# How two attentions of a four-layer graph kernel begin: tile 0's logits and search in a new order, and the second attention's first logits made at the end of the stage ahead

## The chip, the cores and the metric

The kernel runs on one core of a Trainium2 chip. The metric is the time on the device in microseconds (us). The profile is one execution, taken by the hardware profiler; its engines are TensorE (PE, with PEld for its weight loads), VectorE (DVE), ScalarE (ACT), GpSimd (POOL) and SyncE (SP), which issues most of the DMAs.

## The reference

3327 nodes have 256 features each. Four graph layers follow each other, each as `x = layernorm(x + layer(x, adj))`. The change lies in the fourth, which takes two steps of diffusion and of top-p attention:

```python
def top_p_attention(X):                      # W1, W2, W3: 64-wide projections
    q, k = X @ W1.T @ W2.T, X @ W3.T
    probs = softmax(q @ k.T)                 # 3327 x 3327
    sorted by size, row by row: keep an entry while the sum of the larger ones < 0.9
    A = probs * keep
    return A / max(A.sum(-1), 1e-12)
R = (S + I) / rowsum
Xf = Xa = X
for n in range(2):
    A = top_p_attention(Xa)
    Xf, Xa = R @ Xf, A @ Xa
    Z += Xf @ U1[n].T + Xa @ U2[n].T
return layernorm(X + Z)
```

## The kernel before, in words

The nodes are padded to 3328 and lie in `nt` = 26 tiles of 128 rows, with `half` = 1664 columns on either side and `nh` = 13 pairs of tiles. One tile of attention goes through these steps:

- *logits*: `scores` (L1141) makes a row of 3328 logits in four groups. A group is two matmuls (two of 416 columns, from either half of the row) into a PSUM buffer named `sc`, of which there is one, and a copy by ScalarE into the tile `e`. Before that GpSimd sets the one column of padding in `e` (L1146). In the second attention (`p` is 1) matmul and copy are kept in the order in which the program lists them, and each is a step of its own.
- *search*: which entries of `e` are kept. `search_short` (L1390), for the first attention, takes the top 8 of each of 26 segments of 128 (VectorE's MAX8 into `cand`), then six rounds of top 8 and match-replace on these, one exponential over the row by ScalarE after the first round, and the crossing of 0.9, found with a scan. Two maskings of 1664 columns follow. `search_long` (L1424), for the second, finds a cut by sums and counts: two exponentials, then `Relu` and `Sign` passes of ScalarE with an accumulated sum at a first cut c1, again at c2, and scalar steps between them on GpSimd; at c3 VectorE masks into `z`, takes segment maxima, six ranking rounds, the crossing, a match-replace and a masking.
- *products*: the finished `e` is transposed by TensorE, copied by ScalarE into `wt`, and multiplied into an accumulator `acc`. In the first attention two tiles go together with seven products in place of eight (`attended_pair`, with sums of blocks `b` of `X`, for which VectorE makes four of 128 x 1664 into `G`, used there as scratch); in the second one by one (`attended`, L1321).
- *ends*: `first` (L1553) multiplies a tile's result by the U and key matrices: it makes `Y`, the sum `s` (stored to DRAM as `sd`), the tile of `G` for the second attention, and the second attention's keys `kT` and queries `q` (stored as `qd`). `G`'s tile is stored to DRAM (`gd`) too, and read back as a whole into `G` after the first attention, in two loads on SyncE's queue.

Between these lie the products of the diffusion, from blocks of the transposed adjacency (`at`) that SyncE loads: one tile (`diffused_first`, for tile 1, called the x products below), then pairs (`diffused_pair`, with VectorE's subtraction `cb` for each load, and with `own_part`, GpSimd's scaling of a tile of X into `F`), in the second attention tile by tile (`diffused`, L1305, whose `t` and `s` GpSimd adds).

The order on each engine is written out by hand with generators: each of the parts yields after a step, and the main program draws on them in turn. `look` is one step of the oldest search in the queue. At the beginning of the first attention the program draws x products and groups of tile 0's logits by turns; then tile 0's search joins the queue, pair 1's diffusion is begun and its first `at` parts are asked for, and the rest of the x products go with tile 1's logits and two looks each. The loop over pairs follows. The second attention is a loop over `i` from -2 to 26: in round `i` tile `i + 2` has its logits made, tiles `i + 1` and `i` are searched and tile `i - 1` is multiplied. In rounds -2 and -1 there is little or nothing to multiply. Two aids fix an order: `here` and `keep_in_program_order` tie an instruction to its place on its engine; elsewhere a scheduler may move it.

Of the kernel before, what the change touches and what calls it, by code (L numbers as in the profile page):

```python
# [18 lines left out]
P = 128  # L19
# [31 lines left out]
def gnn_kernel(ctx: ExitStack, tc: tile.TileContext, n: int, a: dict, out: bass.AP):  # L51
# [816 lines left out]
    with tc.tile_pool(name="l3", bufs=1) as pool, tc.tile_pool(name="l3d", bufs=1, space=DRAM) as dram:  # L868
# [269 lines left out]
        def in_order(op):  # L1138
            return lambda *x, **k: tc.keep_in_program_order(op(*x, **k))  # L1139

        def scores(work, psum, p, q, e):  # L1141


            copy = in_order(nc.scalar.copy) if p else nc.scalar.copy
            if npad > n:
                nc.gpsimd.memset(e[:, n:], NEG)  # L1146
            halves = e.rearrange("p (h c) -> p h c", h=2)
            for c0 in range(0, half, KC):
                pl = psum.tile([P, 2, 512], F32, name="sc", bufs=1)
                ws = [min(KC, n - c0 - h * half) for h in range(2)]  # L1150

                for h, w in enumerate(ws):
                    k = slice(h * DA, (h + 1) * DA)
                    mm = tensor.matmul(pl[:, h, :w], q[k, :], kT[p][k, c0:c0 + w], start=True, stop=True)  # L1154
# [150 lines left out]
        def diffused(work, atp, psum, p, it, out, each=J3):  # L1305

            rd = rdeg[:, it:it + 1]
            t = work.tile([P, D], F32, name="t")
            nc.gpsimd.tensor_scalar(t, (Y if p else X)[:, it, :], rd, None, op0=ALU.mult)
            if p:  # L1310
                s = work.tile([P, D], F32, name="s")
                nc.sync.dma_start(s, sd[it])
                nc.gpsimd.tensor_tensor(t, t, s, op=ALU.add)
            for acc in aggregated(atp, psum, it, Y if p else X, each):
                if acc is None:
                    yield
            d = work.tile([P, D], F32, name="xf", bufs=DL + 3)
            nc.vector.scalar_tensor_tensor(d, acc, rd, t, op0=ALU.mult, op1=ALU.add)
            out.append(d)

# [61 lines left out]
        def t1(sm, name, w=1):  # L1382
            return sm.tile([P, w], F32, name=name)
# [37 lines left out]
        junks = [None]  # L1421
        edge = [None]

        def search_long(work, sm, e, total, v, kept, halves=False):  # L1424

# [1 line left out]

            def t(name):  # L1430
                return t1(sm, name)

            m8, neg, root = t1(sm, "m8", 8), t1(sm, "neg", 2), t("root")
            nc.vector.max(m8, e[:, :KC])
# [22 lines left out]
            f1, sg, k1, m1 = t("fs1"), t("sg"), t("k1"), t("m1")  # L1457
# [3 lines left out]
            here(nc.scalar.activation(junk, e, AF.Sign, bias=c1, scale=-1.0, accum_out=sg))  # L1461
# [19 lines left out]
            with tc.issue_after(second_cut.ins):  # L1481
# [8 lines left out]
            here(nc.scalar.activation(junk, e, AF.Sign, bias=c2, scale=-1.0, accum_out=sg))  # L1490
            yield
            x, c3 = t("x"), t("c3")
            nc.vector.reciprocal(s, s)
# [59 lines left out]
        def first(work, psum, it, acc, f, xf, tag="pj", xa=None):  # L1553
# [22 lines left out]
            for k in range(2):  # L1576
                tensor.matmul(pg[:, 0, :], xt[:, 2 + k, :], u2[:, 1, k, :], start=(k == 0), stop=(k == 1))
            project_keys(pg[:, 1, :P], it, xt[:, 2:, :])
            g = G[:, it, :] if tag == "pj" else work.tile([P, D], F32, name="s")
            nc.scalar.copy(g, pg[:, 0, :])  # L1580
            if tag != "pj":
                nc.sync.dma_start(gd[it], g)
            store_keys(work, pg[:, 1, :P], 1, it)
            yield
# [70 lines left out]
        with tc.tile_pool(name="l3w", bufs=2) as work, tc.tile_pool(name="l3s", bufs=4) as sm:  # L1655


            def start(p, t, es, searches, search):
                if p or t:
                    q = work.tile([2 * DA, P], F32, name="q")  # L1660
                    nc.sync.dma_start(q, qd[p][t])
                else:
                    q = q0
                es[t] = work.tile([P, npad], F32, name="e", bufs=4)
                searches[t] = search(work, sm, es[t], *(x[p][:, t:t + 1] for x in (tots, vs, kepts)),
                                     **({"halves": True} if p and t == nt - 1 else {}))
                return scores(work, psum, p, q, es[t])

            with tc.tile_pool(name="l3p", bufs=2, space=PSUM) as psum, tc.tile_pool(name="l3a", bufs=1) as quads:
                fixed = True  # L1670
# [56 lines left out]
                        next(todo[r][0])  # L1727
                    ends[0] = todo[0][0]

                groups = logits(0)  # L1730
                x = diffused_first(quads, psum, 1, xfs)
                for _ in groups:
                    next(x)
                queue.append(searches[0])
                spread = spreading(1)
                groups = logits(1)
                for _ in x:
                    next(groups, None)
                    looks(2)
                for _ in groups:  # L1740
                    pass
                queue.append(searches[1])
# [2 lines left out]
                for i in range(nh - 1):  # L1745
                    stage(spread, 7, logits(2 * i + 2), ends, counts,
                          {0: lambda: end_pair(i - 1) if i else None, 5: lambda: attend_to(i), 6: go_on})
                    go_on()
                    counts = [1, 2, 2, 2, 2, 0, 0]
                    queue.append(searches[2 * i + 2])  # L1750
                    values = turned[0]
                    for k in range(7):
                        next(values)
                        looks(k in (1, 2, 4, 5, 6))
                    stage(spread, 6, logits(2 * i + 3), todo[1], [2, 1, 2, 1, 2, 1], {})
                    finish()
# [14 lines left out]
                for it in (nt - 2, nt - 1):  # L1771
# [14 lines left out]
                        pass  # L1786
                    ends = first(quads, psum, it, acc, f, xfs[it], "tp", c)
                    next(ends)
                both(ends)
                fl0 = unresolved(sm, psum, 0)  # L1790
                fixed = False
            for x in (slice(0, JH), slice(JH, nt)):
                nc.sync.dma_start(G[:, x, :], gd[x].rearrange("t p d -> p t d"))

            with tc.tile_pool(name="l3q", bufs=3, space=PSUM) as psum, tc.tile_pool(name="l3at", bufs=3) as atp, \
                    tc.tile_pool(name="l3b", bufs=2) as lone:
                es, searches, xfs = {}, {}, []  # L1800
# [210 lines left out]
```

## Time and profile before

| | |
|---|---|
| median of 3 runs | 3396.89 us (3396.72 to 3399.24) |
| the profiled execution's own time | 3392.58 us |
| its span | 3390.8 us |
| mean granted TensorE clock | 0.967 of full speed |
| instructions | 50286 |

The page's rows are read like this: in the list of engines, the busy time, its share of the span and the number of instructions; in the rows of digits, 40 equal slices of the span, each digit the busy share in tenths (PEclk is the granted clock). The chain of work that ended last has these lines at its head:

```
PE 16%; DVE 4%; ACT 3%; POOL 2%; issue 1%; DMA 0%; SPq 0%; DVEq 0%; POOLq 0%
PE acc L1344 6%; PE acc L1299 6%; PE sc L1154 2%; PE tp L1330 2%; ACT junk L1477 1%; DVE cand L1356 1%; ACT junk L1490 1%; DVE z L1506 1%; DVE e L1535 1%; DVE top L1367 0%; DVE rest L1369 0%; ACT junk L1461 0%; ACT e L1139 0%; DVE e L1543 0
```

It is followed back only to 2557 us. Line 891 is that of a helper which issues the instructions of the first attention; there the tile's name and not the line tells which step it is. In the table of busy time by stretch the columns are the stretch, its length, the busy time of PE, PEld, DVE, ACT and POOL (with the number of instructions in brackets), the granted clock, the DMA engines' busy share and GB/s.

### The profile page before, as it was taken

What the parts mean: (1) busy time and instruction counts of PE and PEld (TensorE: products, weight loads), DVE (VectorE), ACT (ScalarE), POOL (GpSimd) and SP (SyncE); (2) the same over time, 40 slices, a digit from 0 to 9 for tenths busy, and PEclk for the clock granted to TensorE, in tenths of its full rate; (3) what the DMA queues carried; (4) which work ended last, traced back from release to release, by engine and by line L of the source; (5) the groups of instructions that cost most, each with busy time, mean ns of one, the idle gap of its engine ahead of it and who ended that gap; (6) DMA issues with size and microseconds to landing.
All of it is one profiled execution on the core that took longest, in us unless ns stands there. A gap on an engine that the chain in (4) does not pass through costs nothing. (4 is left out here: it accounts for less than half of the span.)

```text
span 3390.8 us, 50286 instructions
## 1 busy us (share of the span) xinstructions
PE 3121.1 (92%) x18301; PEld 2560.0 (75%) x18301; DVE 2692.5 (79%) x5899; ACT 1730.8 (51%) x2763; POOL 1133.6 (33%) x1328
## 2 busy tenths in 40 slices
PE   8999888988888766999979999999997899999997
PEld 5999656666676555888858898898885677777776
DVE  4665268999999998777578878878854899999996
ACT  1000556767667676111133433433436888888883
POOL 0000245656666655111220000000003566666663
PEclk9999999998999888999989999999998999999999
DMA  6775334333343221444322322322313122222221
GB/s 200 250 257 191 112 98 121 114 108 110 103 118 98 63 61 46 167 143 151 118 79 85 89 73 81 89 73 81 89 41 108 42 68 69 66 59 73 72 63 35
DMA packets 206264, 344.31 MB, mean 102 GB/s; under 512 B 22222, under 2 KB 129166, under 8 KB 205870
## 3 DMA queue, kind: packets, MB, share of 16 engines
q1 hardware_dynamic: 205998, 340.92, 33.1%
q8 instruction: 148, 2.42, 0.3%
q14 instruction: 118, 0.97, 0.1%
HBM read 304.65 MB, written 36.21 MB: 101 GB/s over the span
## 5 line engine op out<-in xcount | busy, mean ns | idle before, releaser
L330 POOL TENSOR_TENSOR h<-du,row 128x2048 f32<-128x2048 f32 (+1 forms) x110 | 465.9, 4235 | 344.7 <-DVE hc L330 243.0
L330 DVE TENSOR_TENSOR_SCAN h<-dA,carry,h 128x512 f32<-128x512 f32 (+1 forms) x384 | 448.8, 1221 | 21.7 <-ACT dA L337 21.5
L337 ACT ACTIVATE dA<-t,A_log 128x512 f32<-128x512 f32 (+1 forms) x448 | 292.6, 658 | 147.7 <-DVE h L330 146.0
L1299 PE MATMUL acc<-F,at 128*128 128x256 f32 x1352 | 345.4, 384 | 3.0 <-DMA at<-in_adjT 2.1
L1344 PE MATMUL acc<-G,wt 128*128 128x256 f32 x1352 | 332.6, 388 | 8.6 <-ACT wt L1139 8.3
L1079 PE MATMUL acc<-F,at 128*128 128x257 f32 x1352 | 302.1, 380 | 0.8 <-ACT r L1023 0.8
L389 PE MATMUL cb<-F,at 128*128 128x256 f32 x1196 | 293.0, 393 | 7.6 <-ACT hn L409 3.4
L1344 PEld LDWEIGHTS acc<-G,wt 128*128 128x128 f32 x1352 | 248.9, 191 | 65.3 <-ACT wt L1139 35.5
L1299 PEld LDWEIGHTS acc<-F,at 128*128 128x128 f32 x1352 | 241.8, 191 | 53.6 <-issue 21.5
L1079 PEld LDWEIGHTS acc<-F,at 128*128 128x128 f32 x1352 | 252.4, 190 | 36.1 <-issue 1.1
L680 PE MATMUL y<-ident,hc 128*128 128x128 f32 x1664 | 235.9, 296 | 45.7 <-DVE hc L330 45.5
L1146 POOL MEMSET e<- 128x1 f32 x52 | 4.9, 99 | 816.2 <-PE tp L891 752.5
L680 PEld LDWEIGHTS y<-ident,hc 128*128 128x128 f32 x1664 | 209.4, 153 | 86.6 <-DVE hc L330 62.1
L389 PEld LDWEIGHTS cb<-F,at 128*128 128x128 f32 x1196 | 228.7, 197 | 58.8 <-issue 20.4
L330 DVE TENSOR_TENSOR hc<-h,row 128x2048 f32<-128x2048 f32 (+2 forms) x114 | 243.0, 2133 | 9.7 <-PE y L680 2.6
L891 PE MATMUL acc<-X,at 128*128 128x128 f32 (+1 forms) x988 | 173.7, 287 | 6.1 <-issue 6.1
L1263 ACT COPY wt<-tp 128x512 f32<-128x512 f32 x156 | 90.7, 591 | 167.1 <-PE tp L891 151.7
L138 PE MATMUL acc<-t,cb 128*128 128x128 f32 (+1 forms) x1014 | 168.4, 275 | 0.0
L891 PEld LDWEIGHTS acc<-X,at 128*128 128x128 f32 x988 | 142.3, 194 | 30.1 <-issue 25.3
L891 PE MATMUL acc<-G,sw 128*128 128x128 f32 x936 | 155.5, 275 | 0.0
L1160 ACT COPY e<-sc 128x832 f32<-128x832 f32 x78 | 65.9, 845 | 174.8 <-PE sc L891 174.7
L891 DVE MAX8 cand<-e 128x8 f32<-128x128 f32 x676 | 139.8, 278 | 5.5 <-ACT e L1160 3.7
(417 smaller groups left out, 7273.0 us busy)
## 6 DMA issues: line engine op xcount, KB each, us to landing
at<-in_adjT SPq DMA_DIRECT2D x54, 832.0 KB, 4.4
at<-in_adjT SPq DMA_DIRECT2D x130, 320.0 KB, 3.0
row<-bc SPq DMA_DIRECT2D x80, 512.0 KB, 4.9
at<-in_adjT SPq DMA_DIRECT2D x52, 640.0 KB, 5.3
at<-in_adjT SPq DMA_DIRECT2D x52, 576.0 KB, 4.3
at<-in_adjT SPq DMA_DIRECT2D x72, 256.0 KB, 3.1
at<-mixed SPq DMA_DIRECT2D x72, 256.0 KB, 3.6
mixed<-cb SPq DMA_DIRECT2D x26, 640.0 KB, 3.9
```

The costliest lines, as they stand in the source:

```text
L138: mm = nc.tensor.matmul(acc, w[:, j, :], x, start=(y == 0 and k % 3 == 0 and k < 6), stop=(y == nh - 1 and k in (2, 6)))
L330: return lambda *x, **k: tc.keep_in_program_order(op(*x, **k))
L337: decays.append(op(*x, **k))
L389: ten.matmul(acc, at[:, j % JC, :], X0[:, j, :], start=(j == 0), stop=(j == nt - 1))
L680: x = ten.matmul(y[:, g * P:(g + 1) * P], h[:, g, i * P:(i + 1) * P], ident, is_transpose=True, start=(first and g == 0), stop=(last and g ...
L891: return lambda *x, **k: tc.keep_in_program_order(op(*x, **k))
L1079: nc.tensor.matmul(acc, at[:, j, :], F[:, j0 + j, :], start=(j0 + j == 0), stop=(j0 + j == nt - 1))
L1146: nc.gpsimd.memset(e[:, n:], NEG)
L1160: copy(halves[:, :, c0:c0 + ws[0]], pl[:, :, :ws[0]])
L1263: nc.scalar.copy(wts[-1], pt)
L1299: nc.tensor.matmul(acc, at[:, j, :], rhs[:, j0 + j, :], start=(j0 + j == 0), stop=(j0 + j == nt - 1))
L1344: tensor.matmul(acc, wt[:, j, :], rhs[:, j0 + j, :], start=(j0 + j == 0), stop=(j0 + j == nt - 1))
```

## The change

In the first attention:

- `scores` takes a list of PSUM names; tile 0's groups use `sc` and `acc` by turns. All of its groups are made before the x products; then tile 0's search joins the queue.
- One group of tile 1's logits goes with every second part of the x products, and three looks with every part. Pair 1's diffusion is begun after the x products. So the seven parts hold 21 looks, tile 0's whole search.
- A copy by ScalarE into a small tile `ex` is written ahead of it all.

In the second attention:

- Tile 0's logits are made in the end of the first attention: two steps of them with each step of the last tile's `first`.
- The last four tiles' part of `G` is written by ScalarE straight to its place, without the store to DRAM; the loads of the other 22 are moved ahead of the last pair's ends.
- Rounds -2 and -1 of the loop are replaced by a written list: who takes a step (tile 0's search, tile 1's search, or None for tile 1's logits) and how many diffusion products follow. Products in the list count 26.
- In tile 0's search the two `Sign` passes of ScalarE become counts on VectorE, each in two half passes with an accumulated sum and two small steps.
- The tile `xf` of the diffusion has one more buffer.

```diff
+        def scores(work, psum, p, q, e, banks=("sc",)):
...
+            for k, c0 in enumerate(range(0, half, KC)):
+                bank = banks[k % len(banks)]
+                pl = psum.tile([P, 2, 512], F32, name=bank, bufs=1 if bank == "sc" else 2)
...
+            def signs(c):
+                ks, sg = t1(sm, "ks", 2), t("sg")
+                if counted:
+                    for h in range(2):
+                        z = lone.tile([P, half], F32, name="z", bufs=1)
+                        nc.vector.tensor_scalar(z, e[:, h * half:(h + 1) * half], c, 0.0, op0=ALU.is_gt, op1=ALU.add,
+                                                accum_out=ks[:, h:h + 1])
+                    nc.vector.tensor_add(sg, ks[:, :1], ks[:, 1:])
+                    nc.vector.tensor_scalar(sg, sg, -2.0, float(npad), op0=ALU.mult, op1=ALU.add)
+                else:
+                    here(nc.scalar.activation(junk, e, AF.Sign, bias=c, scale=-1.0, accum_out=sg))
+                return sg
...
-            g = G[:, it, :] if tag == "pj" else work.tile([P, D], F32, name="s")
+            direct = tag == "pj" or it >= nt - 4
+            g = G[:, it, :] if direct else work.tile([P, D], F32, name="s")
             nc.scalar.copy(g, pg[:, 0, :])
-            if tag != "pj":
+            if not direct:
                 nc.sync.dma_start(gd[it], g)
...
-                groups = logits(0)
+                nc.scalar.copy(small.tile([P, 1], F32, name="ex"), eps_t)
                 x = diffused_first(quads, psum, 1, xfs)
-                for _ in groups:
-                    next(x)
+                for _ in logits(0):
+                    pass
                 queue.append(searches[0])
+                groups = logits(1)
+                for k, _ in enumerate(x):
+                    if k % 2 == 0:
+                        next(groups, None)
+                    looks(3)
                 spread = spreading(1)
-                groups = logits(1)
-                for _ in x:
-                    next(groups, None)
-                    looks(2)
...
+                for x in (slice(0, JH), slice(JH, nt - 4)):
+                    nc.sync.dma_start(G[:, x, :], gd[x].rearrange("t p d -> p t d"))
                 end_pair(nh - 2)
...
-                both(ends)
+                es, searches = {}, {}
+                groups = start(1, 0, es, searches, search_long)
+                for _ in ends:
+                    next(groups)
+                    next(groups)
+                both(groups)
...
-            for x in (slice(0, JH), slice(JH, nt)):
-                nc.sync.dma_start(G[:, x, :], gd[x].rearrange("t p d -> p t d"))
...
+                groups = start(1, 1, es, searches, search_long)
+                for t, products in ((0, 0), (0, 0), (None, 0), (None, 4), (0, 0), (None, 0), (None, 4),
+                                    (0, 0), (0, 0), (None, 0), (None, 4), (0, 0), (None, 0), (None, 4),
+                                    (0, 0), (1, 0), (1, 4), (0, 0), (0, 6)):
+                    next(groups if t is None else searches[t], None)
+                    for _ in range(products):
+                        next(spread)
-                for i in range(-2, nt + 1):
+                for i in range(nt + 1):
...
-                    share = iter(range(shares[i - 1] if 0 < i < nt else nt if -2 < i < 1 else 0))
+                    share = iter(range(shares[i - 1] if 0 < i < nt else nt if i < 1 else 0))
```

The instructions on each engine stand in the new order in the two beginnings alone; TensorE has three more of 6381 in the fourth layer. From the first attention's loop over pairs to the last pair's ends, and from the second attention's round 1 on, the order is the same in both.

More of the change, by code (lines that the diff above doesn't have):

```diff
@@ L1139, in in_order @@
             return lambda *x, **k: tc.keep_in_program_order(op(*x, **k))
-        def scores(work, psum, p, q, e):
+        def scores(work, psum, p, q, e, banks=("sc",)):
             copy = in_order(nc.scalar.copy) if p else nc.scalar.copy
@@ L1147, in scores @@
             halves = e.rearrange("p (h c) -> p h c", h=2)
-            for c0 in range(0, half, KC):
-                pl = psum.tile([P, 2, 512], F32, name="sc", bufs=1)
+            for k, c0 in enumerate(range(0, half, KC)):
+                bank = banks[k % len(banks)]
+                pl = psum.tile([P, 2, 512], F32, name=bank, bufs=1 if bank == "sc" else 2)
                 ws = [min(KC, n - c0 - h * half) for h in range(2)]
@@ L1316, in diffused @@
                     yield
-            d = work.tile([P, D], F32, name="xf", bufs=DL + 3)
+            d = work.tile([P, D], F32, name="xf", bufs=DL + 4)
             nc.vector.scalar_tensor_tensor(d, acc, rd, t, op0=ALU.mult, op1=ALU.add)
@@ L1422, in gnn_kernel, with search_long @@
         edge = [None]
-        def search_long(work, sm, e, total, v, kept, halves=False):
+        def search_long(work, sm, e, total, v, kept, halves=False, counted=False):
             def t(name):
                 return t1(sm, name)
+            def signs(c):
[10 more added lines that the diff above has]
+                return sg
             m8, neg, root = t1(sm, "m8", 8), t1(sm, "neg", 2), t("root")
@@ L1456, in search_long @@
             inverse(rc, c1)
-            f1, sg, k1, m1 = t("fs1"), t("sg"), t("k1"), t("m1")
+            f1, k1, m1 = t("fs1"), t("k1"), t("m1")
             yield
@@ L1460, in search_long @@
             yield
-            here(nc.scalar.activation(junk, e, AF.Sign, bias=c1, scale=-1.0, accum_out=sg))
+            sg = signs(c1)
             yield
@@ L1489, in search_long @@
                 scaled(level, c2, float(npad), level, ALU.mult, ALU.add)
-            here(nc.scalar.activation(junk, e, AF.Sign, bias=c2, scale=-1.0, accum_out=sg))
+            sg = signs(c2)
             yield
@@ L1665, in start @@
                 searches[t] = search(work, sm, es[t], *(x[p][:, t:t + 1] for x in (tots, vs, kepts)),
-                                     **({"halves": True} if p and t == nt - 1 else {}))
-                return scores(work, psum, p, q, es[t])
+                                     **({"halves": t == nt - 1, "counted": t == 0} if p else {}))
+                return scores(work, psum, p, q, es[t], ("sc", "acc") if not p and t == 0 else ("sc",))
             with tc.tile_pool(name="l3p", bufs=2, space=PSUM) as psum, tc.tile_pool(name="l3a", bufs=1) as quads:
@@ L1788, in gnn_kernel @@
                     next(ends)
[L1789 removed]
+                es, searches = {}, {}
[4 more added lines that the diff above has]
+                both(groups)
                 fl0 = unresolved(sm, psum, 0)
                 fixed = False
[L1792 to L1793 removed]
             with tc.tile_pool(name="l3q", bufs=3, space=PSUM) as psum, tc.tile_pool(name="l3at", bufs=3) as atp, \
                     tc.tile_pool(name="l3b", bufs=2) as lone:
[L1800 removed]
+                xfs = []
                 result = iter(())
```

## The prediction

> **What bounds the kernel now.** I read the page first, then busy time by stretch, then TensorE's waits at each attention's beginning, then the time lines of the engines that it waits for.
>
> ```profile
> PE 3121.1 (92%) x18301; PEld 2560.0 (75%) x18301; DVE 2692.5 (79%) x5899; ACT 1730.8 (51%) x2763; POOL 1133.6 (33%) x1328
> PE   8999888988888766999979999999997899999997
> PEclk9999999998999888999989999999998999999999
> ```
>
> The first attention runs from 1698 to 2547 us, the second from there to the end. A slice is 84.8 us: in PE's row the two beginnings are slices 21 (7) and 32 to 33 (7, 8), all others of the attentions are 9. Busy time by stretch says it sharper:
>
> ```profile
> 1690.00:1753.00 63.00, 42.74 (x218) 29.79 (x216) 39.72 (x113) 18.44 (x23) 27.25 (x29) 0.88 0.33 100
> 1753.00:2500.00 747.00, 746.62 (x5823) 669.39 (x5823) 615.48 (x2077) 283.22 (x456) 3.31 (x25) 1.00 0.26 77
> 2535.00:2680.00 145.00, 115.95 (x502) 81.70 (x500) 81.81 (x242) 103.29 (x97) 58.39 (x124) 0.91 0.25 78
> 2680.00:3360.00 680.00, 671.66 (x3264) 511.56 (x3263) 622.54 (x1855) 559.76 (x551) 421.69 (x818) 1.00 0.22 65
> ```
>
> The second number is the stretch, the third PE's busy time. After each beginning PE is full, and from there on both kernels issue the same instructions in the same order. So what a beginning gains goes through to the end; it holds 20 us of idle PE in the first, 29 in the second. PE's waits name them:
>
> ```profile
> PE tp L891 <- DVE e L891: 10.1, 2, 8.7
> PE tp L1330 <- DVE e L1543: 12.5, 3, 9.2
> PE sc L1154 <- ACT q L907: 2.3, 1, 2.3
> ```
>
> Columns: total, times, longest. The long waits are those for the first finished weights: tile 0's and 1's e in the first attention (PE idle from 1742.6), tile 0's e in the second (idle from 2607.9).
>
> **First attention, part by part.** The logits of tile 0 take a second PSUM name by turns, and all four groups stand ahead of the x products (tile 1's diffusion), which before waited for the same stream: x's first load lands at 1705. ScalarE's copies (0.85 us each, first at 1700.34) so end at 1703.7 instead of 1717.0. VectorE is in its four products for G until 1708.03; its first 25 segment maxima (0.20 each) end at 1713.1. The 26th needs the padding column, and that is a new gate:
>
> ```profile
> 1690.01 26.22 POOL L1203 TENSOR_SCALAR F<-X,rdeg 128x256 f32<-128x256 f32 x23
> 1716.18 0.18 POOL L1146 MEMSET e<- 128x1 f32 x4
> 1742.64 0.38 DVE L891 MAX8 top<-cand 128x8 f32<-128x208 f32 x1
> 1749.21 1.95 DVE L891 SCALAR_TENSOR_TENSOR e<-e,v 128x1664 f32<-128x1664 f32 x1
> ```
>
> Start, duration, engine. The memset queues behind 23 scalings and ends at 1716.3, hidden before. Tile 0's top then starts at 1716.6, where it was 1720.0. Tile 1's rows give the rest of a search: top 1742.64 to first masking 1749.21 is 6.57 us with one cb subtraction in it, 5.97 without; two maskings (1.87 pitch) follow. Tile 0's search is now whole, ahead of F and cb: 1716.6 + 5.97 + 3.75 and small steps = 1726.6. Then F (0.49) and two cb (0.69 each): 1728.4. Tile 1's maxima take 5.2: 1733.6; 6.57 more: masking from 1740.2, ended at 1742.1 and 1744.0, against 1751.3 and 1753.1. **9.1 us.** ScalarE's copies of tile 1 are done by then, and PE's own work from 1697.9 (11 logits groups at 0.9, 52 products at 0.206, 6 pair products at 1.56: 30 us) would end at 1728 if never kept waiting, so VectorE's chain decides. It keeps PE waiting in new places: pair 1's first product needs cb, now at 1727.7, some 2 us after tile 1's logits, and the fifth needs the third cb at 1736.9, behind two rounds of tile 1's search. PE then ends its queue at 1740.8 and idles 3 us, not 8.7.
>
> Here a clock loss goes too: after the idle from 1742.6 the granted clock was 0.5 from 1747.8 to 1757.5, about 1.9 us of slower matmuls behind 1753. The clock fell 5.2 us after the stop here, 3.7 us after it at 2607.9; a stop of 3 us should not reach it. **11.0 us** in all; bounds 9 (clock lost as before) and 13 (memset no gate).
>
> The copy to "ex", which uses ScalarE before the logits, is placed by the scheduler far ahead, in layer 1; the activation table load stays in front of the first e copy (1699.05 to 1700.33). I cost it at nothing (0.2 us of ScalarE at 51% busy), and it gains nothing.
>
> **Second attention.** Before, after the last tile's U matmuls (2541.12), PE stood 2.28 us for that tile's q (ScalarE first waited 2.33 us at 2546.71 for buffer s, whose reader is a store) and began tile 0's logits at 2547.71, four groups at 2.7 us each through one PSUM buffer; copies ended at 2557.70. Now two groups are issued while PE waits for xt and for F, one each after; the last four tiles' G goes straight to its place, so neither store nor wait is left. With matmul groups of 0.9 and copies of 0.85: groups at 2540.3, 2543.8, 2546.1, 2548.05, e at 2550.0, **7.7 us earlier**. The four stores and their wait are gone; G's load moves ahead on SP's queue, behind the store of tile 21 and nothing later, so nothing behind it stalls. Before, it occupied the DMA engines when the first at block was asked for at 2550.66 (0.94 and 0.92 busy in 2550 to 2560), and that landed at 2559.4; with the queues clear, 3.0 us is the median of such a load: 2553.5.
>
> The search: exponentials (3.07 + 0.19 each) 2550.1, 2554.1 to 2557.3, c1 at 2557.8. Before, Relu waited in ScalarE's order for tile 1's copies until 2569.66, and Sign followed it. Now Relu (2558.05 to 2561.3) runs beside the count on VectorE in two half passes. No row shows this form at that width: the near row is the masking of 128x1664, 1.95 us, the other end the same operation at 128x104, 0.32 us, scaled by width less a fixed 0.16: 2.6. I take 1.95, as it reads one stream to the row's two. Count ends at 2562.3. POOL's steps to c2 took 3.5 us undisturbed (2601.75 to 2605.2): 2565.9. On ScalarE tile 1's exponential now lies ahead of Relu(c2): 2567.2 to 2570.4, and the second count ends with it. Then c3, 2.0 as before, and z at 2573.1 (before 2590.4). z and the maxima took 9.1 us before (2590.38 to 2599.92, less a diffusion row of 0.47): the six ranking rounds start at 2582.3 and five of them are over at 2586.3.
>
> Here comes the wait that takes the place of the removed ones:
>
> ```profile
> 2606.33 0.16 DVE L1493 RECIPROCAL s<-s 128x1 f32<-128x1 f32 x1 [2.03 <-POOL s L1447]
> ```
>
> That reciprocal is tile 1's, stands in VectorE's queue ahead of tile 0's last steps in both kernels, and waits for POOL's s, so for tile 1's exponentials, Relu and Sign on ScalarE. Queued behind it: the crossing, match-replace and masking of tile 0, and PE's transposes behind them. From tile 1's earlier start I work out Sign at 2584.3, c2 at 2588, s behind POOL's t (0.94) at 2590.2; then 10.5 us as before (2606.33 to 2617.05, less a diffusion row): e at 2600.7, **16.3 us earlier**.
>
> That holds with a warm PE. The trace speaks against it:
>
> ```profile
> 2545.00:2550.00 5.00, 1.72 (x11) 0.81 (x11) 0.78 (x4) 1.74 (x4) 0.00 (x0) 0.98 0.21 66
> 2550.00:2555.00 5.00, 3.10 (x10) 0.59 (x8) 0.25 (x1) 1.70 (x2) 2.12 (x3) 0.50 0.94 308
> ```
>
> PE busy 1.72 of 5.00, then clock 0.50, until 2563.8. [...] By the row a thinly used stretch is enough. After the change PE has only two groups and a few projections in 2546 to 2551 and stays as thin. I go by the row: half clock from 2551 to 2563 costs the 16 products among tile 1's logits their 0.206 once more (3.3 us) and the logits some 0.4, so 3.7 us, on tile 1's s, and e is at 2604.4: **12.7 us**. Bounds: 7.7 (only the logits' head start survives) and 19 (no wait at the reciprocal).
>
> Behind tile 0's e the order is the old one. The next waits (59.65 us from there to tile 2's e, through ScalarE's queue) start earlier by the same amount.
>
> **Sum** against the profiled execution, 3392.58 (span 3390.8 and 1.8 around it): 11.0 + 12.7 = 23.7, so 3368.9. It lies 4.3 below the median, 3396.89; the predicted median is 3373.2. The measurement tells 0.2% apart, 6.8 us.
>
> **Rivals.**
> - *Warm* (0.15). PE keeps its full clock in both: 11 + 16.3 to 19, so 27 to 30: 3367 to 3370. [...] Against: the row.
> - *One beginning only* (0.22). The cb held back behind tile 0's search starves the pair products, or PE falls cold and only 9 us or less is left of the first; or in the second tile 1's s stays near 2606.3. Gain 9 to 14: 3383 to 3388. For: each beginning already ends in a wait that the change moves by order alone. Against: the 30 us of PE work leave 12 us of room.
> - *Nothing* (0.06). The shift is absorbed behind: some later chain (the 59.65 us with ScalarE's queue) is bound to what did not move. 3390 to 3397. Against: 746.62 of 747 and 671.66 of 680 busy.
> - *Slower* (0.04): VectorE's reciprocal for tile 1. Tile 1's logits, products and loads start inside cold PE and share ScalarE with tile 0's passes; each us that tile 1's s is late is a us of e. The gain is gone at 2606.3; with the first's 11, the kernel is slower from 2617, and measurably from 2624, 20 us later than worked out at half clock. At 2630 it would be 3410. Against: in the kernel before, with tile 1's loads landing later, it was ready at 2606.3.
>
> **Numbers.** My case has 0.53. Range 3363 to 3387: the low end is both upper bounds (13 + 19 = 32, with 2 for a shared error), the high end a gain of 10. Faster 0.90, same 0.06, slower 0.04.
>
> **What would show it.** Right: tile 0's top in the first attention within 1 us of 1716.6, set by the memset; PE's wait for tile 0's and 1's e 3 us; clock 1.0 in 1740 to 1755; in the second, e's copies done 7 to 8 us earlier, PE at half clock shortly after, VectorE's longest wait at tile 1's reciprocal, tile 0's e at 2604 less the first's 11; PE full behind both. Wrong: a second PSUM buffer that makes PE wait elsewhere, a count pass of over 3 us, or a wait for tile 2's e that grows by what tile 0's lost.

## The result, and the profile after

The changed kernel took 3375.79 us, median of 4 runs (3371.59 to 3379.24); the kernel before, on the same chip, 3396.8 us, median of 4 (3391.59 to 3399.24). The ratio is 0.9943, with a 95% interval of 0.9929 to 0.9956: 15 to 24 us faster, 19.4 in the middle. The forecast was 23.7 us, the time 3373.2 us.

The profiled execution took 3376.88 us with a span of 3375.1, only 15.7 us less than that of before. The reason for the small difference is in front of the change: VectorE's last F row, with which the layers ahead end, starts at 1699.66 us here and at 1697.01 before. Over all traces below it lies between 1692.4 and 1701.6, with nearly the same code ahead of it. So I compare stages, from marks that lie inside the fourth layer.

The page of the changed kernel, the same rows as before:

```profile
PE 3123.7 (93%) x18301; PEld 2564.2 (76%) x18301; DVE 2700.0 (80%) x5911; ACT 1723.8 (51%) x2760; POOL 1127.4 (33%) x1328
PE   8999888988888767899989999999998899999997
PEclk9999998999999888999999999999999999999999
```

PE's busy time is the same to 2.6 us, as nothing was taken from it; what fell is its idle time. The longest waits of PE in the first beginning (1690 to 1900 us), then those in the second (2510 to 2680), with two lines of the kernel before under the first:

```profile
PE sc L891 <- ACT e L1161: 6.4, 2, 4.7
PE acc L891 <- DVE cb L891: 3.9, 1, 3.9
PE acc L891 <- issue: 2.2, 1, 2.2
PE sc L891 <- DVE F L931: 1.2, 1, 1.2
PE tp L891 <- DVE e L891: 0.5, 1, 0.5
...
PE acc L891 <- issue: 6.1, 1, 6.1
PE sc L891 <- ACT e L1160: 3.1, 2, 2.2
```
```profile
PE tp L1331 <- DVE e L1557: 9.3, 3, 4.3
PE acc L1345 <- ACT wt L1139: 4.1, 3, 1.7
PE acc L1300 <- DMA at<-in_adjT: 3.1, 1, 3.1
PE acc L1300 <- issue: 2.8, 1, 2.8
```

The 10.1 us for the first weights are 0.5, and the 6.1 us for the first load of x are 2.2. In their place the wait for ScalarE grew from 3.1 to 6.4, and the 3.9 for cb is new. In the second, the 12.5 us for finished weights became 9.3: tile 0's part fell from 9.2 to 2.2, but tile 1's rose from 0.6 to 2.8 and tile 2's from 2.7 to 4.3. The 2.3 for q are gone.

The stages, each mark taken as a start: F (that last row), sw (the first product with sw), tp (the last tile's transposes from sw), e0 (the first transposes of the second attention's tile 0).

| us | F to sw | sw to tp | tp to e0 | e0 to end |
|---|---|---|---|---|
| before | 62.88 | 780.0 | 77.20 | 773.7 |
| changed | 55.94 | 780.0 | 63.35 | 776.15 |

The middle is equal to 0.1 us, in every trace: what the first beginning gains goes through. In this pair of traces the gain is 6.9 us in the first and 11.4 from tp on: 13.85 at e0, of which 2.45 are lost again behind it.

### The profile page after: what moved, and what is told of

It reads as the page before. It is cut to its first block, busy times and chain, and to the rows that moved or that the text cites. A ratio compares the mean times of both kernels' runs of the same rounds, so it can differ in the third digit from the quotient of the medians.

```text
span 3375.1 us, 50279 instructions
## 1 busy us (share of the span) xinstructions
PE 3123.7 (93%) x18301; PEld 2564.2 (76%) x18301; DVE 2700.0 (80%) x5911; ACT 1723.8 (51%) x2760; POOL 1127.4 (33%) x1328
## 5 line engine op out<-in xcount | busy, mean ns | idle before, releaser
L389 PEld LDWEIGHTS cb<-F,at 128*128 128x128 f32 x1196 | 231.0, 199 | 60.1 <-issue 20.4
L1444 ACT ACTIVATE junk<-e,c 128x3328 bf16<-128x3328 f32 x50 | 154.1, 3083 | 0.0
```

What stands on the lines that cost most here:

```text
L389: ten.matmul(acc, at[:, j % JC, :], X0[:, j, :], start=(j == 0), stop=(j == nt - 1))
L1444: here(nc.scalar.activation(junk, e, AF.Sign, bias=c, scale=-1.0, accum_out=sg))
```

## The experiments

The table gives each kernel's time, and its stages from one trace; e1 to e4, e5 to e8 and e9 to e12 shared a chip each. The scatter of times is such that ratios tell about 4 us apart; the stages of the first attention repeat within 1.4 us with equal code there (54.8 to 56.1).

| | median us | ratio to before, 95% | F to sw | tp to e0 | tp to end |
|---|---|---|---|---|---|
| e1 first part only | 3384.54 | 0.9976 (0.9969 to 0.9983) | 55.16 | 78.11 | 852.9 |
| e2 second part only | 3378.61 | 0.9968 (0.9958 to 0.9978) | 62.04 | 62.49 | 836.4 |
| e3 padding on VectorE | 3369.90 | 0.9937 (0.9924 to 0.9949) | 50.05 | 65.34 | 840.5 |
| e4 x products ahead | 3371.30 | 0.9946 (0.9930 to 0.9961) | 53.15 | 62.85 | 838.0 |
| e5 Sign on ScalarE | 3378.54 | 0.9954 (0.9941 to 0.9967) | 54.81 | 65.44 | 837.0 |
| e6 G by DRAM | 3371.87 | 0.9935 (0.9919 to 0.9951) | 55.53 | 65.27 | 837.3 |
| e7 head start only | 3382.79 | 0.9960 (0.9946 to 0.9974) | 56.11 | 70.12 | 845.8 |
| e8 e3 and e4 together | 3371.03 | 0.9934 (0.9921 to 0.9947) | 49.03 | 64.64 | 839.9 |
| e9 changed again | 3373.17 | 0.9938 (0.9924 to 0.9952) | 56.13 | 62.79 | 837.7 |
| e10 as e8 | 3369.06 | 0.9928 (0.9915 to 0.9941) | 49.19 | 63.11 | 838.5 |
| e11 e8 with Sign | 3368.64 | 0.9924 (0.9909 to 0.9938) | 49.19 | 65.85 | 837.8 |
| e12 table ahead | 3372.78 | 0.9936 (0.9923 to 0.9948) | 54.92 | 62.96 | 838.7 |

### Do the parts add? (e1, e2)

e1 is the changed kernel with the second attention's edits undone, e2 with those of the first.

> Only the first attention's part of the change; the second attention is that of before. Theory: the two parts add. From F's last row in VectorE (end of the layer ahead) to the first product with sw the changed kernel took 55.9 us and the one before 62.4, so this takes 55.9 to 56.5 and ends about 6.5 us below before (ratio 0.998). Rival (the first part is worth what I forecast, and the second gave less): 11 us below before, ratio 0.9968. Rival (the first part only moves the wait): within 2 us of before.

> Only the second attention's part; the first is that of before. Theory: from the last tile's transposes (tp from sw) to the first transposes of tile 0's e 63.4 us as in the changed kernel (before 77.2), to the end of the span 11 to 14 us less than before: ratio 0.996 to 0.9967. Rival (a warm PE or the moved loads need the first part): less than 9 us.

e1 gains 8.1 us (5.8 to 10.5), e2 10.9 (7.5 to 14.2), together 19.0 where the whole gained 19.4. They add, each keeps its stage, and neither "one beginning only" nor "nothing" holds. The first part is worth 7 to 8 us, not 11 (e1's interval, 0.9969 to 0.9983, leaves the rival's 0.9968 just outside).

### Why the first part gave less (e3, e4, e8, e10)

The theory came from the changed kernel's time lines, here of ScalarE, PE, SyncE and VectorE (start, duration, engine, and in square brackets the idle time before and who ended it):

```profile
1719.76 3.07 ACT L1408 ACTIVATE e<-e,neg 128x3328 f32<-128x3328 f32 x1 [8.09 <-POOL F L1204]
1723.71 1.76 PE L891 MATMUL sc<-kT,q 64*128 64x416 f32 x4 [4.74 <-ACT e L1161]
1725.40 4.12 PE L891 MATMUL acc<-X,at 128*128 128x256 f32 x12
1728.69 0.55 SPq L1231 DMA_DIRECT2D at<-in_adjT  x1
1729.92 0.52 SPq L1233 DMA_DIRECT2D at<-mixed  x1
1718.75 0.30 DVE L891 MAX8 cand<-e 128x8 f32<-128x128 f32 x1 [3.23 <-POOL e L1146]
1734.45 0.69 DVE L891 TENSOR_TENSOR cb<-at 128x512 f32<-128x512 f32 x1 [3.81 <-DMA at<-mixed]
```

Read them as a chain. GpSimd's late padding column holds VectorE's last segment maximum, and through top and `neg` (ready at 1719.64) tile 0's exponential. The first row names GpSimd's F row, which ended at 1719.70; that row stands right behind the column and came at the same time. Behind the exponential, in ScalarE's order, stands the second copy of tile 1's logits; so the only sc buffer stays full and the third group of logits waits 4.74 us on PE, with 12 x products behind it. Their `at` buffers come free late, so pair 1's second load is asked for at 1728.7 to 1729.9, and VectorE's second cb waits 3.81 us, with tile 1's search behind it. Two edits cut this chain in two places:

```diff
-                nc.gpsimd.memset(e[:, n:], NEG)
+                (nc.vector if early else nc.gpsimd).memset(e[:, n:], NEG)      # e3: early for tile 0
```
```diff
-                    if k % 2 == 0:
+                    if k in (0, 2):                                            # e4
                         next(groups, None)
```

> The changed kernel, but the padding column of tile 0's e in the first attention is set by VectorE between its products for G and its maxima, not by GpSimd behind 23 scalings. Theory: the memset is the gate of tile 0's top (3.23 us of idle VectorE), and through the exponential also of ScalarE's next copy, of the sc buffer and of the x products queued behind it on TensorE; so all of it comes 3.2 us earlier, the first product with sw 52.8 us after F instead of 55.9, and the time is 3 us below the changed kernel (ratio to before about 0.9934). Rival: the second cb's load sets the pace on its own: nothing (0.9943).

> The changed kernel, but tile 1's last two groups of logits stand behind all of the x products on TensorE instead of between them; nothing else is moved but one copy on ScalarE, now behind the exponential. Theory: the x products stood behind a group of logits that waited 4.74 us for ScalarE; their loads' buffers came free late, so pair 1's second load was asked for at 1728.7 and VectorE's second cb waited 3.81 us for it. Without that the load is asked for 9 us earlier, the cb waits for nothing, tile 1's search is 4.2 us earlier, the first product with sw 51.8 us after F, the time 4 us below the changed kernel (ratio about 0.9931). Rival (the load is slow by itself, from DMA contention): the cb waits 3 to 4 us still, no gain. Rival (the logits' copies are late instead): tile 1's maxima wait for ScalarE, gain under 1 us.

VectorE in e3, then in e4:

```profile
1706.77 0.06 DVE L1146 MEMSET e<- 128x1 f32 x1
1706.95 4.91 DVE L891 MAX8 cand<-e 128x8 f32<-128x128 f32 x25
...
1724.71 0.69 DVE L891 TENSOR_TENSOR cb<-at 128x512 f32<-128x512 f32 x1 [1.69 <-DMA at<-mixed]
```
```profile
1713.08 0.30 DVE L891 MAX8 cand<-e 128x8 f32<-128x128 f32 x1 [3.22 <-POOL e L1146]
...
1723.84 1.28 DVE L891 TENSOR_TENSOR cb<-at 128x512 f32<-128x512 f32 x2
```

In e3 the maxima run through and the wait for the load falls to 1.69 us: F to sw is 5.9 us shorter than in the changed kernel. That is more than the 3.2 I expected, since the load comes earlier with it (2.1 us less wait). In e4 the gate is still there (3.22 us), but both cb run together without a wait: tile 1's search was over 46.5 us after F, where the changed kernel took 51.0. That is 4.4 us, where 4.2 were expected; at sw 2.8 of them are left. The other 1.6 went to the clock: from the end of that search to sw e4 took 6.6 us, the changed kernel 5.0, and in e4 the granted clock was 0.50 from 1742.5 to 1745.0, just when the weights were transposed; VectorE's second and third sw waited 1.87 and 1.34 us for ScalarE's wt there, 0.94 and 0.65 in the changed kernel. The chain is shown in both places by the traces; the ratios alone (0.9937, 0.9946) could not tell either kernel from the changed one.

> The changed kernel with both mendings in the first attention: the padding column set by VectorE, and tile 1's last two groups of logits behind the x products. From F to the first product with sw the changed kernel took 55.9 us, with the column alone 50.1, with the order alone 53.2. Theory (both act on one chain: the order only takes away what is left of the wait for pair 1's second load, 1.69 us): 48.4 to 49 us, about 7 us below the changed kernel, ratio to before 0.992 to 0.993. Rival (additive): 47.3. Rival (TensorE's own work is the bound by then): 50, as with the column alone.

> Both mendings in the first attention once more (padding column on VectorE, logits behind the x products), on the same chip as the changed kernel. Theory: F to the first product with sw 49 us against 55 to 56, so 6 to 7 us less than the changed kernel, 0.998 of it. Rival (the gain is lost behind): equal.

Both together: 49.0 and 49.2 us, so they act on one chain and do not add: 6.9 and 6.75 us less than the changed kernel, where 5.9 and 2.8 would make 8.7. Against e9 on the same chip e10 is 4.1 us faster in the median and 6.9 in the stage; the intervals of the ratios overlap, so it is by the stage that this version is the better one.

### The table load (e12)

`ex` reads the first queries, so that its copy stands behind them and takes the table load:

```diff
-                nc.scalar.copy(small.tile([P, 1], F32, name="ex"), eps_t)
+                nc.scalar.copy(small.tile([P, 1], F32, name="ex"), q0[:, 0:1])
```

> The changed kernel, but the copy to ex reads the first queries, so that it stands right behind them on ScalarE, and the activation table is loaded with it instead of with the first copy of e. Theory (forecast: worth nothing): the table load is over 2 to 4 us earlier and the four copies of tile 0's e 1.3 us, but VectorE is in its products for G until 5 us after that; F to sw as in the changed kernel, 55 to 56 us. Rival (the copies gate the second use of sc and so the x products): 1.3 us less.

ScalarE in e12 (F is at 1697.21 there):

```profile
1697.67 1.28 ACT L1745 ACT_TABLE_LOAD   x1 [2.16 <-issue]
1698.96 0.19 ACT L1745 COPY ex<-F 128x1 f32<-128x1 f32 x1
1699.35 0.85 ACT L1161 COPY e<-sc 128x832 f32<-128x832 f32 x1 [0.20 <-POOL F L1204]
```

The first copy is 2.1 us behind F instead of 3.5, and F to sw is 54.9, within the 54.8 to 56.1 of the others. As forecast the load hides behind VectorE's work: tile 0's last segment maximum, with the padding column as its gate, starts 19.1 us behind F in both. In the changed kernel `ex` itself ran at 1341.3 us and did nothing; the load stayed in front of the first copy, at 1701.88.

Behind that maximum the two traces differ, though the sum comes out alike. In e12 the second cb waits 1.59 us and not 3.81, and tile 1's e is ready 48.3 us behind F (51.0 in the changed kernel), but from there to sw it is 6.6 us and not 5.0. e6, whose first attention is that of the changed kernel, does the same without the early table load (2.29, 48.9 and 6.6), so it is not the table; by the durations told below, the half clock fell at other places.

### What carries the second part (e5, e6, e7, e11)

e5 calls tile 0's search with `"counted": False`. e6 puts back the stores of G's last four tiles and both loads behind the attention. e7 drops the written list and the counts: the loop runs from -2 again, with no logits made in round -2.

> The changed kernel, with tile 0's two counts in the second attention back as Sign passes of ScalarE behind Relu. Theory (ScalarE's queue is the path): the first count ended before Relu did, so each Sign puts 3.27 us and a copy's place in front of tile 0's next cut and of tile 1's passes behind it; z of tile 0 comes some 6 us later, tile 1's s too, and from the last tile's transposes to tile 0's e it is 69 to 70 us instead of 63.4; the time 5 to 6 us above the changed kernel (ratio to before 0.9959). Rival (the reciprocal of tile 1 sets e anyway): e 3 us later or less, ratio 0.995. Rival (VectorE's counts cost as much as they save): no difference.

> The changed kernel, with all of G stored to DRAM and loaded behind the first attention, as before. Theory: ScalarE's copy of the last tile waits again for a store (2.3 us), which delays the last group of tile 0's logits by as much, and the load of G occupies the DMA engines when the first at block is asked for, so that block lands 4 to 5 us later after its request; tile 0's e comes 3 to 5 us later (66.4 to 68.4 us from the last tile's transposes), ratio to before 0.9952 to 0.9958. Rival (the loads hide behind the search): within 1 us of the changed kernel in this stretch.

> The changed kernel, but in the second attention only tile 0's early logits and the way of G are kept: the loop of before makes rounds -2 and -1, and the counts are Sign passes again. Theory: the head start of the logits (7.5 us in the trace) goes through to e nearly whole, and the earlier landing of the at block gives some more: 68 to 70 us to tile 0's e where before had 77.2 and the changed kernel 63.4; ratio 0.9955 to 0.996. Rival (the written list and the counts do it all): 74 us or more, ratio 0.9975.

> Both mendings, and the counts of tile 0 in the second attention as Sign passes of ScalarE again. In the traces the Sign passes cost tile 0's e 2.75 us but tile 3's e nothing (156.4 us behind the last tile's transposes, others 155.8 to 159.8). Theory: the counts bring nothing to the end, since behind e of tile 0 the waits for tile 1's and 2's take what it gained; equal to the kernel with both mendings within 2 us, tile 3's e at 155 to 158. Rival (the counts are worth their 2.75 us): 3 us slower.

e7 came as expected: 70.1 us to e0 and 845.8 to the end, 6.1 less than the mean of the two traces with the old second part (851.9). The rest, down to 838.7 (the mean of the eight traces with the changed second part), comes with the list and the counts together. Which of these, e5 and e11 tell: with Sign passes e0 is late by 2.75 us once the start of Relu is taken into account (46.2 us behind Relu against 43.4), but the end is not: 837.0 and 837.8 against 836.4 to 840.5. Tile 1's e is late too (94.0 and 94.3 us behind tp, against 88.8 to 92.4), but by tile 2's the difference is gone (123.6 and 124.0, against 121.3 to 125.5). On one chip, e11 took 3368.64 us and e10 3369.06, the fastest two of all. So the counts moved tiles 0 and 1 alone. At e0 the rival came true (3 us or less, as tile 1's reciprocal sets e anyway), not my 5 to 6 us, and my forecast of a use for the counts was wrong, too. e5's own times, with a ratio of 0.9954, would leave room for a cost of some 4 us; its trace and e11 show none.

Where the gain goes, the traces show at tile 3. Its Sign pass at the first cut starts 1.8 us earlier behind tp with the counts (110.0 us in the changed kernel, 111.8 in e5). But GpSimd begins its steps to tile 3's second cut at 115.5 and 115.1 us: in the changed kernel a diffusion step stands ahead of them in its order, which waited 4.99 us for VectorE's `xf`. What comes of this cut is tile 3's reciprocal. It stands ahead of tile 2's last masking on VectorE, which waits 1.68 us for it in the changed kernel; e5 shows no such wait.

e6's first product after tile 1's first logits, in PE's time line:

```profile
2548.34 3.75 PE L1300 MATMUL acc<-F,at 128*128 128x256 f32 x8 [5.63 <-DMA at<-in_adjT]
```

That wait was 2.85 us in the changed kernel; the block was asked for 10.8 us behind tp in e6 and 10.4 there, and in the two stretches of 5 us from there the DMA engines were busy 84% and 100% in e6 (from 2540), 65% and 32% in the changed kernel (from 2545). So the load of G does collide with the first at block, and Relu of tile 0 starts 24.2 us behind tp instead of 19.9. Yet e0 is at 65.3, ahead of the 66.4 to 68.4 expected, and the end at 837.3. The scheduler also put other numbers of products between the logits in e6, so it is no clean removal of G's way alone; in the whole it gains nothing that these runs can show. The list without the counts is what remains for the last 7 us: e5 differs from e7 by the list, and its stage to the end is 8.8 us shorter (837.0 against 845.8), though the two ratios, 0.9954 and 0.9960, do not tell them apart. The list alone, without the direct G, was not tried.

### The scatter of tile 0's e (e9)

> The changed kernel once more, beside the three below. From the traces so far: F to the first product with sw 54.8 to 56.1 us, the last tile's transposes to tile 0's e 62.5 to 65.3, from there to the end of the span 771.5 to 776.2. Theory: the distance to tile 0's e follows how long TensorE is at half clock after the last logits of the first attention's end, as Relu of tile 0 does (e is 43.4 to 44.0 us behind Relu in all traces with this code); ratio 0.9935 to 0.995. Rival (something else moves e): e is not 43.4 to 44.0 us behind Relu.

With one and the same code in this stretch, tp to e0 is between 62.5 and 65.3 us. Relu of tile 0 tells why. It stands in ScalarE's order behind a copy of tile 1's logits, and that copy waits for PE, here in e2 and in e3:

```profile
2552.79 0.85 ACT L1139 COPY e<-sc 128x832 f32<-128x832 f32 x1 [0.99 <-PE sc L1155]
2546.56 0.85 ACT L1139 COPY e<-sc 128x832 f32<-128x832 f32 x1 [3.34 <-PE sc L1155]
```

| us behind tp | e2 | e9 | e4 | e12 | e10 | changed | e8 | e3 |
|---|---|---|---|---|---|---|---|---|
| full clock is back | 16.5 | 17.0 | 17.2 | 17.3 | 17.5 | 18.4 | 19.7 | 20.4 |
| Relu starts | 19.09 | 19.38 | 19.44 | 19.52 | 19.67 | 19.91 | 20.67 | 21.44 |
| e0 | 62.49 | 62.79 | 62.85 | 62.96 | 63.11 | 63.35 | 64.64 | 65.34 |
| e0 less Relu | 43.40 | 43.41 | 43.41 | 43.44 | 43.44 | 43.44 | 43.97 | 43.90 |

The first row comes from the clock in steps of 2.5 us, and the first three rows rise together from left to right. (In e8 and e3 tile 0's e was ready 43.3 us behind Relu as well; PE, busy with other products, came to it 0.6 us later.) So e0 follows the time at which the full clock comes back. It does not follow how long PE is at half clock, as I had expected: that was 6.8 us in e4, e12 and e10 and only 3.4 us in the changed kernel, yet its e0 comes later than theirs.

In e3, the stretch behind tp (2525.9) in steps of 2.5 us (the third column from the end is the clock):

```profile
2535.00:2537.50 2.50, 1.18 (x6) 0.30 (x4) 0.00 (x0) 2.16 (x3) 1.40 (x2) 1.00 0.29 75
2537.50:2540.00 2.50, 0.00 (x0) 0.00 (x0) 0.00 (x0) 2.50 (x3) 1.66 (x3) 0.89 0.91 302
2540.00:2542.50 2.50, 2.17 (x5) 1.84 (x6) 0.59 (x1) 2.50 (x2) 0.82 (x4) 0.50 0.61 213
2542.50:2545.00 2.50, 2.50 (x8) 1.49 (x7) 1.23 (x1) 0.71 (x2) 1.62 (x4) 0.50 0.00 0
2545.00:2547.50 2.50, 2.50 (x9) 1.32 (x10) 2.46 (x3) 0.94 (x2) 0.00 (x0) 0.75 0.56 161
```

PE stands still while its at block lands, and then works at half clock just when tile 1's logits are due: (0.11 + 0.50 + 0.50 + 0.25) of 2.5 us, times two, is 6.8 us of it.

## Why the prediction was right, and where it was off

Direction and range held, and so did most of the mechanism. The gain was 19.4 us by the ratio, 20.2 by the mean stages (first: 62.5 less 55.5 us; second: 851.9 less 838.7), where 23.7 was forecast. Two steps failed in the first attention, and a third held only nearly.

**First attention: 11.0 forecast, 7.0 measured.** The first half of the chain held to half a microsecond once the later start (F is 2.65 us later) is added: top at 1719.08 (worked out 1719.25), set by the memset with VectorE idle for 3.23 us; first masking 1725.17 (1725.2); first cb 1729.96 (1729.75). Then the step failed that reads "Then F (0.49) and two cb (0.69 each): 1728.4": it took the second cb's load as landed. It was asked for at 1729.9 and cost 3.81 us, so that tile 1's e was ready at 1750.6 and not at 1746.65. From F to tile 1's e this made 51.0 us against 56.0 before, a gain of 5.1 and not 9.1. I had named the memset as a gate of VectorE and stopped there; I did not follow it to ScalarE's next copy, the single sc buffer and the products queued behind on PE. The bound of 13 for "memset no gate" was near: with the memset alone out of the way e3 gained 62.5 less 50.05, so 12.4 us, and with the order as well e10 gained 13.3.

**The clock there: 1.9 forecast, 1.9 measured, by luck.** "A stop of 3 us should not reach it" failed as well; the stops were longer, 4.74 us and 3.86 us. PE in the changed kernel, by stretch:

```profile
1716.00:1721.00 5.00, 2.98 (x14) 2.28 (x12) 2.08 (x9) 1.24 (x1) 3.70 (x8) 1.00 0.35 93
1721.00:1726.00 5.00, 2.29 (x6) 1.01 (x7) 4.34 (x15) 3.48 (x5) 0.00 (x0) 0.52 0.12 41
1738.00:1743.00 5.00, 1.68 (x16) 1.49 (x14) 4.79 (x23) 2.48 (x2) 0.00 (x0) 0.86 0.50 156
1743.00:1748.00 5.00, 4.46 (x15) 3.05 (x16) 4.41 (x13) 1.60 (x4) 0.00 (x0) 0.50 0.06 22
```

The half clock came twice, earlier than before, and was over when the weights were ready (the clock was 0.95 from 1748 to 1753). So from tile 1's e to sw it took 5.0 us and not the 6.9 of before, as forecast, but not because the clock stayed up: in e4 the half clock fell behind tile 1's e (0.50), and this piece took 6.6 us there, as in e6 and e12. Nor was it free where it fell. In the changed kernel the third group of tile 1's logits took 1.76 us and the 12 x products behind it 4.12; in e6 and e12 the same group took 0.97 us, and pair 1's second load was asked for 26.9 and 27.0 us behind F instead of 29.0. So part of the 3.81 us wait is the clock's, and what one place of the half clock saves is nearly lost at the other: F to sw is 54.8 to 56.1 in all seven traces with this order.

**Second attention: 12.7 forecast, 13.2 measured to the end.** The head start was 7.5 us against 7.7 (e's last copy 10.3 us behind tp, before 17.8). The count took 1.95 us a half pass, as taken from the masking's row:

```profile
2553.51 1.95 DVE L1439 TENSOR_SCALAR_CACHE_REDUCE z<-e,c 128x1664 f32<-128x1664 f32 x1 [2.99 <-POOL c L1461]
2588.03 0.16 DVE L1507 RECIPROCAL s<-s 128x1 f32<-128x1 f32 x1 [2.14 <-POOL s L1461]
```

And the second row is the wait that I said would take the place: tile 1's reciprocal, 2.14 us. It starts 52.4 us behind tp, between the 50.3 worked out for a warm PE and the 54.0 for a cold one, and so at e0 the gain was 13.9 in the profiled pair, between the warm 16.3 and the cold 12.7. The clock did fall after the thin stretch (PE busy 1.19 us of 2545 to 2550 in the changed kernel), as in the row of before, but for 3.4 us (changed) or 6.8 us (e3) instead of 12. The copies in ScalarE's order pass it on, so that it shows at Relu already, 20 us behind tp, and not only at tile 1's s.

**"Behind tile 0's e the order is the old one."** The order held, but "earlier by the same amount" held only nearly: e0 to tile 2's e is 60.7 us in the changed kernel, 59.65 before, and e0 to the end is 775.2 us in the mean of the eight traces with the changed second part, 774.2 in the two with the old one. So of 14.2 us at e0, in the mean, 1.0 was lost again, and that 13.2 came so close to 12.7 is in part that e0 did better than forecast and what lies behind it worse. The sentence also hides that a gain for the first tiles alone is not a gain for the kernel: with Sign passes the e of tiles 0 and 1 was later and tile 2's not.

**The rivals.** Warm fell to the half clock, if to less of it than feared. One beginning only and nothing fell to e1 and e2. Slower needed tile 1's s behind 2624; it came at 2588. (2624 is 30 us behind the 2593.9 worked out at half clock, not 20.)

**The signs.** Come true: the memset as tile 0's gate, e's copies 7.5 us earlier, half clock shortly after, PE full behind both beginnings. Not come true: the wait for tile 0's and 1's e was 0.5 us and not 3, since PE reached it late; the clock was 0.50 from 1743 to 1748; and the wait at tile 1's reciprocal was not VectorE's longest there (3.9 us for GpSimd's c at the second count was). Of the signs of being wrong, PE did wait elsewhere in the first attention, though not through the second PSUM name, and tile 2's wait grew by 1.6 us of the 7.0 that tile 0's lost. Two readings were slips without weight: the thin slices of the second beginning are the 31st and 32nd of PE's row, and 2606.33 to 2617.05 less a diffusion row is 10.3 us, not 10.5.

## What to carry to other kernels

Where a change makes a new gate (here a memset of 0.1 us behind 26 us of unhurried work), follow what waits for it through every in-order queue, buffer ring and load request, to the end; the second and third engine can cost more than the first. Before giving work to a faster place for the first tile of a pipeline, ask when the third tile is due: here a gain for the first two alone was taken back by the next waits. When run-to-run scatter is as large as the effect, take marks inside the program, and compare stages.

## What the runs showed of the hardware

In e2 and e4 the granted clock fell to half without any single stop over 2.3 us. In e2 PE's longest stop in the stretch behind tp was 2.27 us, and the clock was 0.61 from 12.5 us behind tp on. In e4 the clock fell at about 2537.5, and the longest stop behind tp until then was 1.01 us:

```profile
2534.70:2537.20 2.50, 1.03 (x6) 0.30 (x4) 0.43 (x3) 1.43 (x3) 0.00 (x0) 1.00 0.10 26
2537.20:2539.70 2.50, 1.76 (x4) 0.50 (x4) 0.00 (x0) 2.42 (x2) 2.12 (x3) 0.57 0.48 142
```

And the time at half clock fell near three values in the 14 traces. Summed from the clock in steps of 2.5 us over the 22.5 us from 5 us behind tp, it is 3.4 to 3.5 us in the changed kernel, e2, e5, e7 and e9, 6.8 to 6.9 in e3, e4, e8, e10, e11 and e12, and 13.7 in the kernel before, e1 and e6: once, twice, four times 3.4. So with the same code in this stretch the half clock lasted 3.4 us in the changed kernel and e9, and 6.8 us in e3, e4 and e12; what decides between the two no run here shows.

GpSimd's scaling of 128x256 took 0.93 us, but up to 3.82 us beside VectorE's four products for G (1702.80 to 1710.68 in the changed kernel). The same scaling, from 1692 to 1702 and from 1703 to 1710 us (busy time, mean ns of one):

```profile
L1204 POOL TENSOR_SCALAR F<-X,rdeg 128x256 f32<-128x256 f32 x11 | 9.9, 932 | 0.0
L1204 POOL TENSOR_SCALAR F<-X,rdeg 128x256 f32<-128x256 f32 x4 | 8.9, 2244 | 0.0
```

The 23 scalings ahead of the padding column took 26.0 us, where 23 times 0.93 is 21.4. An estimate from these numbers: at that pace the column would have come 4.6 us earlier, at 1714.0, ahead of the end of the other maxima (1715.5), and would have been no gate at all.
